# Values of two blocks of keys at a time, ahead of scores, in a two-layer graph attention kernel on one core

## Chip, cores, metric

One core of one Trainium2 chip runs the whole program. The metric is the device time of the execution in microseconds (us), lower is better. PE is the matrix engine (TensorE), DVE the vector engine (VectorE), ACT the scalar engine (ScalarE), POOL the GpSimd engine, SP the engine that issues most DMAs.

## What is computed

Thirty-two graphs of 512 nodes with 512 features go through two layers. The first is a graph sum with two weight matrices, the second is attention with 8 heads of 64, masked by the adjacency matrix. In the kernel's names B is 32, N and D are 512. After each layer the input is added and the rows are normalised.

```python
# layer 0, a = adj as float, deg its row sums
mi = einsum('bkd,od->bko', x, Wi); mj = einsum('bkd,od->bko', x, Wj)
x  = layernorm(x + deg[None, :, None] * (mi + b) + einsum('ij,bjo->bio', a, mj))
# layer 1
q, k, v = heads(h @ Wq.T + bq), heads(h @ Wk.T + bk), heads(h @ Wv.T + bv)
scores  = where(adj == 0, -inf, q @ k.T / sqrt(64))
x  = layernorm(h + merge(softmax(scores) @ v) @ Wo.T + bo)
```

## The kernel before

**Pieces.** Each 512 x 512 weight product is computed by a Strassen-like scheme with seven half-size products ("pieces", `piece`, line 411), numbered 1, 2, 6, 7, 4, 5, 3. The sums of activations that they need are made on POOL by `combos` (line 387); the sums of weights lie in DRAM and come through a ring of seven tiles (`prefetch`, line 274, on SP). A piece is eight 128 x 128 by 256 matrix instructions into one PSUM bank, `mma` or `mmb`; a layer-0 piece ("l0") is twice as long, since it has two weights. The pieces of one product fall into groups that add up in the bank: X is pieces 1 and 2, Y is 6, 7 and 4, Z is 5 and 3. After each piece but the first of a product its bank is read by DVE (`xh`, L445; `v`, L456; `q` and `k`, L465 and L472) or ACT (L454, L470 for piece 2); after the first ACT copies it (`p`, L434). Each bank is single, so the next piece into the same bank waits for that read, whether it adds into the group or opens a new one. This is why the lists alternate between two banks. Kinds: l0 (layer 0), v, q, k, pj (output projection). `l0_gather` (L325) multiplies by the adjacency matrix.

**Attention of one batch row b.** Its eight heads are two groups g of four, and keys are four blocks kc of 128, so a row takes eight steps (`STEPS`). For a step, `scores` (line 477) is called twice, for two heads each: a PSUM tile `sc` of two banks (two such tiles exist), `exp` on ACT in place (L485), then the multiplication by the 0/1 adjacency mask into an SBUF tile `e` on DVE (L486, "the mask"; four `e` tiles exist). `values` (line 496) multiplies the four heads' `e` of one block of keys by v into the two PSUM tiles `ov`. `presum` (line 488) adds the `e` of the four blocks on POOL (kc 1) or DVE (kc 2, 3). At the end of a group `sums` (line 506) makes the row sums with a matrix product into an `sc` tile, `drain` (line 515) copies them to SBUF on ACT, and `rest` (line 540) is seven DVE instructions: four inversions (`invert`, L522), two `scale` (L538, which also frees the `ov` tiles), and one `tell` (L526), a sum for a check.

**Forms of matrix instructions.** By the profile's columns pieces use the array as 128\*128, scores as 64\*128 (two heads side by side), values and sums as 128\*32 (four heads side by side).

**Order.** Nothing is left to a scheduler: under `tc.manual_schedule()` each engine's queue holds its instructions in the order in which the Python code emits them. Period n works on several rows at once: attention of row n-1, layer 0 and q, k, v of row n, the projection of row n-2 (m), and the gather of row n+1. The lists `phase_b`, `phase_c` and `phase_a` hold the pieces and the small tasks between them; `by_steps` (line 684) cuts them into eight steps. With n from 2 to 30 step 0 has l0-2, pj-1, l0-6, pj-2; step 1 l0-7, pj-6, l0-4, pj-7; step 2 l0-5, pj-4, l0-3, pj-5; step 3 v1, pj-3, v2, q1, k1, q2; step 4 k2, q5, v5, q3, v3; step 5 six pieces of q and v; step 6 gathers and k5, k3, k6; step 7 a gather, k7, l0-1, k4. l0, v and k share one bank, pj and q the other; in the gathers' steps the next period's bank for l0 is used.

The loop of the periods (line 765) does, for each step: scores of the step, values of the step before, at a group's end sums, drain and then `rest` kept in `extra`; then the pieces of the step, with the presums and `extra` handed out between them (in step 0 all of `extra` after the first piece, otherwise one or two instructions after each).

**h.** The output h of layer 0 is needed transposed. `stats` (DVE, POOL) and `apply` (ACT, L296) normalise half of the rows, `h_store` (line 356) sends the half to DRAM from ACT's queue, `h_load` (line 362) fetches it with four DMAs on SP's queue, `h_turn` (line 370) transposes it on DVE (L373) into `HT`, from which v, q and k are made. Pieces 1 and 2 of these need only half 0.

Of the kernel before, what the change touches and what calls it, by code (L numbers as in the profile page):

```python
# [25 lines left out]
def gnn_attention_kernel(  # L26
# [37 lines left out]
    B, N, D = x.shape  # L64
    NC = N // P
# [14 lines left out]
    def work(shape, name, bufs, dtype=FT):  # L80
        return pools.work.tile(shape, dtype, name=name, bufs=bufs)
# [7 lines left out]
    def ov_tile():  # L89
        return psum.tile([P, 512], FT, name="ov", bufs=2)  # L90

    def sc_tile():
        return psum.tile([P, 2, N], FT, name="sc", bufs=2)
# [147 lines left out]
    def ring_tile():  # L241
        return work([P, 2, Q], "ring", RING)
# [31 lines left out]
    def prefetch():  # L274
        while len(TILES) < min(len(KEYS), ring.used + RING) and KEYS[len(TILES)] in WS:
            t = ring_tile()
            nc.sync.dma_start(t, WS[KEYS[len(TILES)]])
            TILES.append(t)
# [102 lines left out]
    def quarter(src, j, n):  # L381
        return src[:, 2 * j:2 * j + 2, Q * n:Q * n + Q]

    def ot_quarter(b):
        return lambda j, n: OT[b, j][:, :, Q * n:Q * n + Q]
# [91 lines left out]
    def scores(b, hp, kc):  # L477
        ps = sc_tile()
        for s in range(2):
            r = slice(s * HD, (s + 1) * HD)  # L480
            nc.tensor.matmul(ps[:, s, :], KT[b, hp // 2][r, hp % 2, kc * P:(kc + 1) * P],  # L481
                             QT[b, hp // 2][r, hp % 2, :], start=True, stop=True)
        e = E[hp % 2, kc] = work([P, 2, N], "e", 4)

        nc.scalar.activation(ps, ps, AF.Exp, scale=QSCALE)  # L485
        nc.vector.tensor_tensor(e, ps, edge[:, kc:kc + 1, :].to_broadcast([P, 2, N]), op=OP.mult)  # L486
# [9 lines left out]
    def values(b, g, kc):  # L496

        if kc == 0:
            PV[g] = [ov_tile(), ov_tile()]
        for r in range(2):  # L500
            for h in range(4):
                c0 = (4 * g + h) * HD + 32 * r
                nc.tensor.matmul(PV[g][r][32 * h:32 * h + 32, :], V[b][:, kc, c0:c0 + 32], E[h // 2, kc][:, h % 2, :],  # L503
                                 start=(kc == 0), stop=(kc == NC - 1))

    def sums(g, kcs=(1,), last=1):

        if g not in RL:
            RL[g] = (sc_tile()[:, 0, :], work([P, N], "rl", 1))
        for kc in kcs:  # L510
            for h in range(4):
                src = ES[h // 2] if kc == 1 else E[h // 2, kc]
                nc.tensor.matmul(RL[g][0][32 * h:32 * h + 32, :], ones[:, :32], src[:, h % 2, :], start=(kc == 1), stop=(kc == last))  # L513

    def drain(b, g):

        j = 2 * (b * 2 + g)
        nc.scalar.activation(RL[g][1], RL[g][0], AF.Identity, accum_out=told[:, j:j + 1])
# [21 lines left out]
    def rest(b, g):  # L540
        return [(invert, g, c) for c in range(4)] + [(scale, b, g, 0), (scale, b, g, 1), (tell, b, g)]
# [9 lines left out]
    def z(f, *a):  # L551
        return (0.0, f, *a)

    def pc(kind, b, i, bank):
        return (2 * PC if kind == "l0" else PC, piece, kind, b, i, bank)
# [6 lines left out]
    def banks(n):  # L562

        return ("a", "b") if n % 2 == 0 else ("b", "a")
# [48 lines left out]
    def project(m, i):  # L613

        res = [pc("pj", m, i, banks(m)[1])]
        if i == 1:
            res = [z(combos, TO, m, ot_quarter(m), (1,))] + res
        if i == 2:
            res = [FLUSH] + res + [z(combos, TO, m, ot_quarter(m), (2, 3, 4))]
        return res  # L620

    def phase_b(n):

        m = n - 2
        if m < 0:
            res = []
            side = [z(add_bo, 0, i) for i in range(2)]
            A, K = banks(n)
            for i, bank in ((2, A), (6, K), (5, A), (7, K), (4, K), (3, A)):
                res.append(pc("l0", n, i, bank))  # L630
                if i == 4:
                    res += [z(stats, n, 0)]
                res += side[:1]
                side = side[1:]
            return res + [z(apply, n, 0), z(stats, n, 1), (TR, l0_norm, n, 0), (TR, l0_norm, n, 1)]
        A = banks(n)[0]
        l0 = {i: pc("l0", n, i, A) for i in ORDER}
        return [l0[2], *project(m, 1), l0[6], *project(m, 2), l0[7], z(add_bo, n - 1, 0), *project(m, 6), l0[4], z(stats, n, 0),
                *project(m, 7), z(apply, n, 0), z(h_store, n, 0), l0[5], z(h_load, n, 0), z(add_bo, n - 1, 1), *project(m, 4),
                l0[3], z(stats, n, 1), z(h_turn, n, 0), *project(m, 5)]  # L640

    def phase_c(n):

        m = n - 2
        norm = [(TR, l0_norm, n, ic) for ic in range(NC)]
        h = lambda j, i: quarter(HT[n], j, i)
        A, K = banks(n)
        v, q, k = [{i: pc(kind, n, i, bank) for i in ORDER} for kind, bank in (("v", A), ("q", K), ("k", A))]
        if m < 0:
            res = [v[1]] + ([z(apply, n, 1)] if n else []) + [q[1], v[2], norm[2], norm[3], z(combos, TH, n, h, (1, 2)), k[1],  # L650
                                                             z(combos, TH, n, h, (3, 4)), q[2], k[2]]
        else:
            res = [z(apply, n, 1), z(h_store, n, 1), v[1], *project(m, 3), z(h_load, n, 1), z(stats, m, 0), v[2], z(stats, m, 1),
                   q[1], k[1], z(apply, m, 0), z(h_turn, n, 1), q[2], z(apply, m, 1), z(store, m),
                   z(combos, TH, n, h, (1, 2)), z(combos, TH, n, h, (3, 4)), k[2]]
        side = []
        if n == 0:

            side = [z(graph_forms, 2), None, z(graph_forms, 0), None, z(graph_forms, 1)]
        for i in LATE:  # L660
            for f in q[i], v[i]:
                res += [f] + [g for g in side[:1] if g]
                side = side[1:]
                if i in (6, 7) and 0 < n < B - 1:
                    res += [z(load_xa, n + 1, 2 * (i == 7) + (f is v[i]))]
            if i == 3 and 0 < n < B - 1:
                res += [z(load_x, n + 1)]
            if i == 7 and n + 1 < B:
                res += [z(ahead, n + 1)]
        return res  # L670
# [35 lines left out]
    def run(f):  # L706
        f[1](*f[2:])
# [29 lines left out]
    def flags():  # L737
# [5 lines left out]
        nc.vector.tensor_scalar(again, tot, -1.0, 1.0, op0=OP.mult, op1=OP.add)  # L743

    PERIODS = [first() + phase_c(0) + phase_a(1)]
    half = None
    for n in range(1, B):
        todo = phase_b(n) + phase_c(n) + phase_a(n + 1)
        if n < B - 1:
            half = sum(f[0] for f in todo) / 2  # L750

        PERIODS += [by_steps(todo, half)]
# [8 lines left out]
    for f in PERIODS[0]:  # L761
        run(f)
        if f[1] is combine:
            prefetch()
    for n in range(1, B + 1):
        b = n - 1
        extra = []
        for step in range(STEPS):
            g, kc = divmod(step, NC)
            scores(b, 2 * g, kc)  # L770
            scores(b, 2 * g + 1, kc)
            pb, pg, pk = (b, *divmod(step - 1, NC)) if step > 0 else (b - 1, 1, NC - 1)
            if pb >= 0:
                values(pb, pg, pk)
                if pk == NC - 1:
                    sums(pg, *(((1, 3), 3) if pb == B - 1 else ()))
                    drain(pb, pg)
                    extra = rest(pb, pg)
            late = [(presum, i, kc) for i in range(2) if kc > 0]
            if b == B - 1 and kc > 2 - g:  # L780

                late = []
            for f in PERIODS[n][step]:
                if f is FLUSH:
                    some = len(extra)
                else:
                    run(f)

                    some = 0 if f[0] == 0.0 else len(extra) if step == 0 else max(1, round(f[0] / PC))
                if some:  # L790
                    for g in late[:1] + extra[:some]:
                        g[0](*g[1:])
                    late, extra = late[1:], extra[some:]
            for g in late + extra:
                g[0](*g[1:])
            extra = []
# [19 lines left out]
    with tc.If(flag > 0), tc.tile_pool(name="general", bufs=1) as pools.work:  # L816
# [26 lines left out]
        with tc.For_i(0, B, 1) as b:  # L843
            g = "general"
# [105 lines left out]
```

## Time and profile before

| | us |
|---|---|
| median of 3 runs (3705.42 to 3707.18) | 3706.04 |
| the profiled execution | 3703.08 |
| its span | 3701.0 |
| PE busy | 3664.3 |
| DVE busy | 2390.7 |
| POOL busy | 1938.8 |
| ACT busy | 1028.4 |

The page gives, for each engine, the sum of its instructions' times and their share of the span. The timeline lists instructions in order: start, length, engine, line, operation, what it writes and reads, the number of merged instructions, and in brackets the idle time ahead and what ended it. PE's ends are modelled and overlap the next start, so its rows are best read from start to start. A line of the windows view is one stretch of time: its length, then each engine's busy time with its number of instructions, the granted clock of PE, the DMA share and the rate. One period takes 113.4 us, and its pattern is the same from period 2 on, but for the two banks, which swap.

### The profile page before, as it was taken

The numbers are of one execution on the slowest core, as the hardware profiler recorded it, in microseconds if no ns is written. First come the engines' busy times: TensorE is split into PE (matmuls) and PEld (weight loads), VectorE is DVE, ScalarE is ACT, GpSimd is POOL, SyncE is SP. The second block draws the span as 40 slices with busy tenths as digits, with TensorE's granted clock in tenths as the row PEclk, the third lists the DMA queues.
The fourth block names the chain that finished last, engine by engine and source line by source line (L and its number), as shares of the span: only waits on it lengthen the run. The fifth ranks groups of instructions, "written<-read, shape, count | busy, mean of one in ns | idle before, by whom it ended". The sixth has DMA issues, their size and how long they took to land.

```text
span 3701.0 us, 49651 instructions
## 1 busy us (share of the span) xinstructions
PE 3664.3 (99%) x18474; PEld 2511.5 (68%) x18474; DVE 2390.7 (65%) x3134; ACT 1028.4 (28%) x1482; POOL 1938.8 (52%) x1985
## 2 busy tenths in 40 slices
PE   8999999999999999999999999999999999999998
PEld 5666666666676767676767666666666676767663
DVE  4566766666666666666666666666666666666665
ACT  2222232322322222222232222232222322222322
POOL 3465545555455564455554555545555545555443
PEclk9999999999999999999999999999999999999999
DMA  7444555455564445554555544555544556445541
GB/s 250 127 126 134 151 151 162 122 143 137 154 159 142 128 135 151 157 155 125 137 143 157 159 135 134 137 149 160 148 132 132 147 151 164 124 136 140 151 137 47
DMA packets 797173, 530.02 MB, mean 143 GB/s; under 512 B 530432, under 2 KB 611840, under 8 KB 796928
## 3 DMA queue, kind: packets, MB, share of 16 engines
q1 hardware_dynamic: 780384, 494.78, 49.7%
q10 hardware_dynamic: 16320, 31.46, 2.3%
q8 instruction: 151, 2.47, 0.3%
q14 instruction: 94, 0.77, 0.1%
q0 software_dynamic: 224, 0.53, 0.0%
HBM read 453.25 MB, written 73.40 MB: 142 GB/s over the span
## 4 chain that ended last, share of the span: by engine, by line
PE 96%; DVE 1%; SPq 1%; POOL 1%; DMA 0%; issue 0%; ACT 0%; POOLq 0%; DVEq 0%; ACTq 0%
PE mma L427 31%; PE mmb L427 31%; PE sc L481 13%; PE ov L503 13%; PE mmb L325 3%; PE mma L325 3%; PE sc L513 2%; SPq L113 0%; DVE rl L522 0%; DVE e L486 0%; DMA wv<-e 0%; SPq L144 0%; DVE st L289 0%; PE sc L727 0%; POOL es L492 0%
## 5 line engine op out<-in xcount | busy, mean ns | idle before, releaser
L485 ACT ACTIVATE sc<-sc 128x1024 f32<-128x1024 f32 x512 | 493.2, 1007 | 1552.5 <-PE sc L481 1546.2
L486 DVE TENSOR_TENSOR e<-sc,edge 128x1024 f32<-128x1024 f32 x512 | 602.2, 1217 | 206.3 <-ACT sc L485 174.3
L427 PE MATMUL mmb<-ring,big 128*128 128x256 f32 x3144 | 731.7, 381 | 0.0
L427 PE MATMUL mma<-ring,big 128*128 128x256 f32 x3112 | 725.3, 382 | 4.2 <-ACT p L434 3.1
L427 PEld LDWEIGHTS mmb<-ring,big 128*128 128x128 f32 x3144 | 592.0, 190 | 131.5 <-issue 26.8
L427 PEld LDWEIGHTS mma<-ring,big 128*128 128x128 f32 x3112 | 586.3, 190 | 135.2 <-issue 26.0
L396 POOL TENSOR_TENSOR big<-big 128x512 f32<-128x512 f32 x376 | 492.7, 1338 | 32.4 <-ACT big L354 11.7
L481 PE MATMUL sc<-q,k 64*128 64x512 f32 x2048 | 509.1, 615 | 0.0
L503 PE MATMUL ov<-e,v 128*32 128x512 f32 x4096 | 492.5, 598 | 4.9 <-DVE oT L538 4.9
L492 POOL TENSOR_TENSOR es<-e 128x1024 f32<-128x1024 f32 x128 | 300.0, 2355 | 351.7 <-DVE e L486 351.7
L427 PE MATMUL mma<-big,ring 128*128 128x256 f32 x1808 | 430.3, 381 | 3.2 <-DVE k L465 3.2
L427 PE MATMUL mmb<-big,ring 128*128 128x256 f32 x1776 | 422.8, 381 | 1.0 <-DVE v L456 1.0
L291 POOL TENSOR_SCALAR mv<-mv 128x1 f32<-128x1 f32 x256 | 49.6, 194 | 671.6 <-DVE mv L290 659.1
L427 PEld LDWEIGHTS mma<-big,ring 128*128 128x128 f32 x1808 | 340.5, 190 | 76.5 <-issue 26.0
L427 PEld LDWEIGHTS mmb<-big,ring 128*128 128x128 f32 x1776 | 334.4, 190 | 73.4 <-issue 26.0
L503 PEld LDWEIGHTS ov<-e,v 128*32 128x32 f32 x4096 | 107.0, 109 | 352.2 <-issue 320.8
L204 POOL TENSOR_TENSOR xlo<-xh,xhi 128x512 fp32r<-128x512 f32 x128 | 163.6, 1289 | 337.6 <-ACT xhi L203 337.6
L481 PEld LDWEIGHTS sc<-q,k 64*128 64x128 f32 x2048 | 176.1, 186 | 207.3 <-issue 205.1
L340 POOL TENSOR_TENSOR big<-big,deg_r 128x512 f32<-128x512 f32 x124 | 173.6, 1400 | 266.3 <-DVE big L339 266.3
L494 DVE TENSOR_TENSOR es<-es,e 128x1024 f32<-128x1024 f32 x250 | 304.2, 1217 | 0.0
L445 DVE TENSOR_TENSOR xh<-xh,mma 128x512 f32<-128x512 f32 x186 | 126.6, 681 | 267.0 <-PE mma L427 267.0
L445 DVE TENSOR_TENSOR xh<-xh,mmb 128x512 f32<-128x512 f32 x186 | 126.7, 681 | 263.0 <-PE mmb L427 263.0
(155 smaller groups left out, 3656.2 us busy)
## 6 DMA issues: line engine op xcount, KB each, us to landing
ring<-wo SPq DMA_DIRECT2D x217, 256.0 KB, 2.8
ring<-wq SPq DMA_DIRECT2D x160, 256.0 KB, 3.9
ring<-wv SPq DMA_DIRECT2D x160, 256.0 KB, 3.4
ring<-wk SPq DMA_DIRECT2D x160, 256.0 KB, 3.2
ring<-wi SPq DMA_DIRECT2D x155, 256.0 KB, 2.7
ring<-wj SPq DMA_DIRECT2D x155, 256.0 KB, 2.7
xh<-in_x_dram SPq DMA_DIRECT2D x32, 1024.0 KB, 5.4
xa<-in_x_dram SPq DMA_DIRECT2D x124, 256.0 KB, 4.0
```

What stands on the lines that cost most here:

```text
L204: nc.gpsimd.tensor_sub(lo, xs, hi.bitcast(FT))
L325: nc.tensor.matmul(pm, parts[w][:, jc, :], adjR[:, jc, :], start=(w == 0 and jc == 0), stop=(w == 1 and jc == NC - 1))
L340: nc.gpsimd.tensor_tensor(XD[b][:, dc, :], XD[b][:, dc, :], deg_r, op=OP.mult)
L396: nc.gpsimd.tensor_tensor(dst, p, q, op=OP.subtract)
L427: nc.tensor.matmul(pm[:, c * Q:(c + 1) * Q], lhs, rhs, start=first, stop=(kc == 1 and n == len(terms) - 1), skip_group_check=True)
L445: nc.vector.tensor_tensor(d, d, pm, op=OP.add)
L481: nc.tensor.matmul(ps[:, s, :], KT[b, hp // 2][r, hp % 2, kc * P:(kc + 1) * P], QT[b, hp // 2][r, hp % 2, :], start=True, stop=True)
L485: nc.scalar.activation(ps, ps, AF.Exp, scale=QSCALE)
L486: nc.vector.tensor_tensor(e, ps, edge[:, kc:kc + 1, :].to_broadcast([P, 2, N]), op=OP.mult)
L492: nc.gpsimd.tensor_add(ES[i], E[i, 0], E[i, 1])
L494: nc.vector.tensor_add(ES[i], ES[i], E[i, kc])
L503: nc.tensor.matmul(PV[g][r][32 * h:32 * h + 32, :], V[b][:, kc, c0:c0 + 32], E[h // 2, kc][:, h % 2, :], start=(kc == 0), stop=(kc == NC - 1))
```

## The change

Three edits. In `phase_b`, `apply` and `h_store` of half 0 stand ahead of the piece pj-7 instead of behind it. In `phase_c`, pj-3 and the load of half 1 stand ahead of v1, and the order of the following pieces is v1, q1, v2, q2, k1, k2 (it was v1, v2, q1, k1, q2, k2, with pj-3 behind v1), with the small tasks at other places between them. In the loop, the values of two steps are kept in `due` and done together in every second step (kc 0 and 2), ahead of that step's scores; at a group's end (steps 0 and 4) sums, drain and all of `rest` are emitted there too, ahead of the scores and so ahead of their masks. In the last period, steps 1 to 7 (`alone`) keep the old order.

```diff
         return [l0[2], *project(m, 1), l0[6], *project(m, 2), l0[7], z(add_bo, n - 1, 0), *project(m, 6), l0[4], z(stats, n, 0),
-                *project(m, 7), z(apply, n, 0), z(h_store, n, 0), l0[5], z(h_load, n, 0), z(add_bo, n - 1, 1), *project(m, 4),
+                z(apply, n, 0), z(h_store, n, 0), *project(m, 7), l0[5], z(h_load, n, 0), z(add_bo, n - 1, 1), *project(m, 4),
                 l0[3], z(stats, n, 1), z(h_turn, n, 0), *project(m, 5)]
...
-            res = [z(apply, n, 1), z(h_store, n, 1), v[1], *project(m, 3), z(h_load, n, 1), z(stats, m, 0), v[2], z(stats, m, 1),
-                   q[1], k[1], z(apply, m, 0), z(h_turn, n, 1), q[2], z(apply, m, 1), z(store, m),
+            res = [z(apply, n, 1), z(h_store, n, 1), *project(m, 3), z(h_load, n, 1), v[1], z(stats, m, 0), q[1], z(stats, m, 1),
+                   v[2], q[2], z(apply, m, 0), z(h_turn, n, 1), k[1], z(apply, m, 1), z(store, m),
                    z(combos, TH, n, h, (1, 2)), z(combos, TH, n, h, (3, 4)), k[2]]
...
+    due = []
     for n in range(1, B + 1):
         b = n - 1
         extra = []
         for step in range(STEPS):
             g, kc = divmod(step, NC)
-            scores(b, 2 * g, kc)
-            scores(b, 2 * g + 1, kc)
-            pb, pg, pk = (b, *divmod(step - 1, NC)) if step > 0 else (b - 1, 1, NC - 1)
-            if pb >= 0:
-                values(pb, pg, pk)
-                if pk == NC - 1:
-                    sums(pg, *(((1, 3), 3) if pb == B - 1 else ()))
-                    drain(pb, pg)
-                    extra = rest(pb, pg)
+            alone = b == B - 1 and step > 0
+            if alone:
+                scores(b, 2 * g, kc)
+                scores(b, 2 * g + 1, kc)
+            if alone or kc % 2 == 0:
+
+                for pb, pg, pk in due:
+                    values(pb, pg, pk)
+                    if pk == NC - 1:
+                        sums(pg, *(((1, 3), 3) if pb == B - 1 else ()))
+                        drain(pb, pg)
+                        extra = rest(pb, pg)
+                due = []
+            due.append((b, g, kc))
+            if not alone:
+
+                for f in extra:
+                    f[0](*f[1:])
+                extra = []
+                scores(b, 2 * g, kc)
+                scores(b, 2 * g + 1, kc)
             late = [(presum, i, kc) for i in range(2) if kc > 0]
```

## The prediction

> **What bounds the kernel now.** I read the page's first and fourth parts, then one block's stretch, then PE beside DVE in order of time. TensorE is busy for 99% of the span and is 96% of the chain that ended last:
>
> ```profile
> PE 3664.3 (99%) x18474; PEld 2511.5 (68%) x18474; DVE 2390.7 (65%) x3134; ACT 1028.4 (28%) x1482; POOL 1938.8 (52%) x1985
> ...
> PE 96%; DVE 1%; SPq 1%; POOL 1%; DMA 0%; issue 0%; ACT 0%; POOLq 0%; DVEq 0%; ACTq 0%
> ```
>
> A busy PE could still hide waits, so I took the stretch of one block of batch (it repeats every 113.4 us):
>
> ```profile
> 904.44:1017.88 113.44, 113.44 (x581) 78.47 (x577) 74.33 (x97) 31.90 (x46) 60.67 (x64) 1.00 0.53 144
> ```
>
> PE is busy for the whole 113.44 us; DVE for 74.33. So PE waits for nobody in a block, and only two things can move the time: fewer PE cycles, or a new wait of PE. In PE's timeline I read starts only (ends are modelled):
>
> ```profile
> 941.89 1.89 PE L427 MATMUL mmb<-ring,big 128*128 128x256 f32 x8
> 943.71 1.99 PE L481 MATMUL sc<-q,k 64*128 64x512 f32 x8
> 945.63 1.92 PE L503 MATMUL ov<-e,v 128*32 128x512 f32 x16
> 947.49 1.99 PE L427 MATMUL mma<-ring,big 128*128 128x256 f32 x8
> 949.32 1.89 PE L427 MATMUL mmb<-ring,oT 128*128 128x256 f32 x8
> ...
> 959.96 1.92 PE L503 MATMUL ov<-e,v 128*32 128x512 f32 x16
> 961.70 1.04 PE L513 MATMUL sc<-es,ones 128*32 128x512 f32 x8
> 962.67 1.99 PE L427 MATMUL mma<-big,ring 128*128 128x256 f32 x8
> ```
>
> A piece (8 records) takes 1.73 us in a run of pieces, 1.82 before scores and 1.83 after values. Scores take 1.92, values 1.86 before a piece but 1.74 before sums, which use the same 128*32 form; sums 0.97. Each change of form costs about 0.1 to 0.2 us. DVE's timeline shows what a group's end costs there: four inversions, two scales and a sum (L526), 908.81 to 914.02, is 5.21 us in one run; two masks (L486) take 2.27 to the next start (1002.74 to 1005.01), an eviction 0.69:
>
> ```profile
> 908.81 3.38 DVE L522 RECIPROCAL rl<-rl 128x128 f32<-128x128 f32 x4
> 912.22 1.29 DVE L538 TENSOR_TENSOR oT<-ov,rl 128x512 f32<-128x512 f32 x2
> 913.43 0.67 DVE L526 TENSOR_REDUCE told<-rl 128x1 f32<-128x512 f32 x1
> 914.02 0.68 DVE L445 TENSOR_TENSOR xh<-xh,mma 128x512 f32<-128x512 f32 x1
> ...
> 942.09 0.69 DVE L445 TENSOR_TENSOR xh<-xh,mma 128x512 f32<-128x512 f32 x1 [1.63 <-PE mma L427]
> ...
> 945.68 0.65 DVE L445 TENSOR_TENSOR xh<-xh,mmb 128x512 f32<-128x512 f32 x1
> 946.26 2.34 DVE L486 TENSOR_TENSOR e<-sc,edge 128x1024 f32<-128x1024 f32 x2
> ...
> 963.53 0.95 DVE L522 RECIPROCAL rl<-rl 128x128 f32<-128x128 f32 x1 [0.91 <-ACT rl L518]
> ```
>
> The first inversion starts 1.83 us after sums start (961.70 to 963.53); between them is ACT's drain. Last, what a late eviction does to PE is seen in period 1, where a piece follows another into the same bank:
>
> ```profile
> 133.06 3.72 PE L427 MATMUL mma<-ring,big 128*128 128x256 f32 x16
> 137.56 3.72 PE L427 MATMUL mma<-ring,big 128*128 128x256 f32 x16 [0.78 <-DVE xh L445]
> ```
>
> The double piece takes 3.45 (3.55 after a change of form or a stop), so 136.61 was due; the eviction, 136.81 to 137.50, held it to 137.56: 0.06 after the eviction's end.
>
> [...] the eviction at 914.02 stood behind the seven instructions since 908.81. [...] the waits below are up to 2.1 us, and the block's clock is 1.00, so I price no throttling.
>
> **The change, part by part.**
>
> *Fewer changes of form.* Two steps now hold pieces, values, values, scores, pieces, scores, pieces: five changes instead of six. An entry into values and an exit go. The exit is 1.86 - 1.74 = 0.12; the entry about 0.02 (1.74 against four passes of 0.43). The new neighbours (pieces to values, values to scores) are not in the trace; bounds 0.10 and 0.20 a pair, I take 0.15. With 31 blocks of four pairs: 124 x 0.15 = -19 us (-12 to -25).
>
> *Inversions ahead of masks.* In steps 0 and 4, PE now does values, values, sums, scores. From the step's start: values at 0 and 1.74, sums 3.47, scores 4.44, pieces 6.36. The second scores reuse the PSUM slot of sums, so they wait for the drain, which ends about 1.8 after sums start (5.27); they are due near 5.4: no cost, at most 0.1. DVE's queue is now seven instructions of the group's end, then masks, then the evictions of pieces. Inversions start at 3.47 + 1.83 = 5.30, the end is 5.21 later, 10.51, masks are done at 12.78, and only then the first DVE eviction starts. Before, masks came first and the inversions lay after or between pieces' evictions.
>
> Step 0, n = 2 to 31: l0-2 (double) 6.36 to 9.91, pj1 to 11.64, then l0-6 opens a new tile in l0-2's bank. That eviction is 12.78 to 13.47, so l0-6 starts at 13.53: 1.89 late, and 0.10 for starting again, 1.99. 30 x 1.99 = +60 us.
>
> Step 4, n = 1 to 31: k2 6.36 to 8.19, q5 to 9.92, v5 to 11.65, then q3 adds into q5's bank. q5's two-part eviction (0.87) is 12.78 to 13.65, q3 starts at 13.71: 2.06 late, 2.16 with the restart. v5 waits only for k2's eviction, which ACT does behind two exponentials (to 7.5) and two normalisations, until about 9.9: just in time. 31 x 2.16 = +67 us. If q3's first half waits only for the eviction's first half, 0.44 less: 53.
>
> *h stored sooner, used one piece later.* The store half 0 now stands on ACT ahead of step 2's exponentials; the load on SP is where it was, after l0-5 and its prefetches, which in this trace is what it follows (937.39, 0.7 after l0-5), not the store. So it gains nothing. But pj3 is moved to be the first piece of step 3, while pj5 is the last of step 2, in the same bank and group. DVE has, from pj5's start at 941.89: l0-3's eviction, four statistics, h's transpose, then pj5's eviction, ending 946.33, 4.44 later. Before, v1 in the other bank stood between. Now step 3 has no values, so pj3 is due at 1.82 + 1.92 = 3.74 and may start at 4.50: 0.76 late. 30 x 0.76 = +23 us. If the transpose waits longer for its DMA, more; if statistics were earlier, nothing. The second half's load keeps its distance from its store (7.96 after step 3's start), and its transpose (ending some 1.7 into step 4) lies ahead of the inversions that wait till 5.30. k1 and k2 in one bank are parted by values and scores: nothing.
>
> *Cover that values gave.* Step 7 loses 1.86 us of values. DVE has masks, a transpose, two bias additions, a presum, then k7's eviction, ending 9.24 after scores start (1000.52 to 1009.76). k4 in that bank is due at 1.92 + 1.96 + 1.73 + 3.45 = 9.06, may start at 9.30: 0.24 + 0.10 = 0.34 late. 29 x 0.34 = +10 us; between 0 and 1 us each. In steps 1 and 5 the same sum leaves 0.2 us and more in hand.
>
> *Tail.* Step 0 of the last period has one piece; step 1's scores need the first mask, about 11.8 after the start against 8.3 due: 3.5, where before a wait of 1.2 stood (3623.17). +2.
>
> Everything else is equal: same pieces, same prefetch, the presums end before the masks that overwrite their inputs (GpSimd done some 8 us earlier by my count).
>
> Sum: 60 + 67 + 23 + 10 + 2 - 19 = +143. The profiled execution took 3703.08 us around a span of 3701.0; 3703 + 143 = 3846. The median of the runs is 3 us above it: 3849.
>
> **Rivals.**
>
> *Half of it (0.17).* Evictions release PE by halves and steps 3 and 7 have more slack than counted: 60 + 53 + 2 - 19 = +96, 3802. For: step 7's 0.24 us is within small shifts. Against: 946.33 and 1009.76 are chains without an idle moment.
>
> *More of it (0.15).* The late masks are passed on: the drain holds the second scores and step 1's and 5's pieces meet a still late DVE, 1 us more at each of 61 group ends: +61, 3910. For: DVE has only 39 us free in a block. Against: in steps 1 and 5 masks are due 2.2 after scores, when the evictions left over are one or two.
>
> *The other side (0.05): DVE isn't late.* If the group's end lies in DVE's idle time, all stops vanish and the drains saved are left: 3706 - 19 = 3687. It decides if masks are done 2.1 us sooner, that is if the end takes 3.1 us instead of 5.21, and pj5's and k7's evictions come 0.8 sooner. For: DVE is busy only 65%. Against: the inversions cannot start before 5.30, and 5.21 is a row of the trace. The drain alone can't turn the sign: all changes of form of two steps are 2 x 0.53 = 1.06 us, 131 us in all, under the 160 of stops.
>
> *The change doesn't do what it says (0.03).* If the queue isn't the program's order, masks pass the inversions and little is left, about 3706. Every DVE row above stands in program order.
>
> **How the numbers follow.** The forecast has 0.60; its own range is 3815 to 3885 (each stop 0.3 either way, drain 12 to 25). The range 3785 to 3900 takes in the half case and a part of the larger one. A measurement of this kernel can tell about 0.2%. Slower: 0.60 + 0.17 + 0.15 and a little of the rest, 0.93; faster 0.05; same 0.02.
>
> **What would show it.** Right: in steps 0 and 4, seven DVE instructions ahead of L486; an idle PE of about 2 us at l0-6 and at q3, released by L445 and L472; 0.8 at pj3; values 1.74 apart. Wrong: a block still without idle PE, or a block not near 113.4 + 4.6 = 118 us.

## The result, and the profile after

The changed kernel takes 3898.69 us (3897.76 to 3901.96, 5 runs) against 3706.29 us of the kernel before on the same chip: a ratio of 1.0522, 95% interval 1.0507 to 1.0536. It is slower, as forecast, and by more than the 3849 us that were forecast; the time lies just inside the upper edge of the range, 3900.

The page after, parts 1 and 4:

```profile
PE 3705.9 (95%) x18474; PEld 2535.8 (65%) x18474; DVE 2382.9 (61%) x3134; ACT 1035.9 (27%) x1482; POOL 1950.2 (50%) x1985
...
PE 58%; DVE 19%; POOL 14%; issue 5%; ACT 2%; SPq 1%; DMA 1%; DVEq 0%; POOLq 0%; ACTq 0%
```

PE runs the same 18474 instructions, is now idle for about 5% of the span, and the chain that ended last goes through DVE and POOL for a third of it. Two of PE's numbers have to be read together: the span grew by 195.9 us, PE's busy time grew too, by 41.6. So there is more than waiting: some instructions take longer.

Two neighbouring periods in the windows view (length, busy times of PE, PEld, DVE, ACT, POOL, clock, DMA share, GB/s):

```profile
945.60:1065.67 120.07, 115.39 (x578) 79.70 (x577) 74.10 (x97) 32.16 (x46) 61.11 (x63) 0.99 0.49 136
1065.67:1183.90 118.23, 113.53 (x577) 78.52 (x576) 74.10 (x97) 32.16 (x46) 60.98 (x62) 1.00 0.50 138
```

Both were 113.4. The second line ends 0.16 us before its period does (the next pair of values starts at 1184.06), so the period takes 118.39 us; the first has 1.7 us more, and the clock of PE isn't 1.00 in it. First the stops, that is, the times in which PE waits. PE's timeline after, step 3's start, then step 4, with its pair of values, sums and scores ahead:

```profile
993.08 1.99 PE L481 MATMUL sc<-q,k 64*128 64x512 f32 x8
995.76 1.99 PE L427 MATMUL mmb<-ring,oT 128*128 128x256 f32 x8 [0.69 <-DVE xh L445]
...
1006.32 3.64 PE L503 MATMUL ov<-e,v 128*32 128x512 f32 x32
1009.77 1.04 PE L513 MATMUL sc<-es,ones 128*32 128x512 f32 x8
1010.75 2.01 PE L481 MATMUL sc<-q,k 64*128 64x512 f32 x8
1012.68 1.99 PE L427 MATMUL mma<-big,ring 128*128 128x256 f32 x8
1014.51 1.89 PE L427 MATMUL mmb<-big,ring 128*128 128x256 f32 x8
1016.24 1.89 PE L427 MATMUL mma<-ring,big 128*128 128x256 f32 x8
1020.08 3.47 PE L427 MATMUL mmb<-big,ring 128*128 128x256 f32 x8 [1.95 <-DVE q L472]
1023.34 2.15 PE L427 MATMUL mma<-ring,big 128*128 128x256 f32 x8
```

DVE's timeline beside it (the brackets give the idle time ahead and what ended it):

```profile
1011.60 3.39 DVE L522 RECIPROCAL rl<-rl 128x128 f32<-128x128 f32 x4 [2.87 <-ACT rl L518]
1015.09 1.29 DVE L538 TENSOR_TENSOR oT<-ov,rl 128x512 f32<-128x512 f32 x2
1016.30 0.68 DVE L526 TENSOR_REDUCE told<-rl 128x1 f32<-128x512 f32 x1
1016.89 2.35 DVE L486 TENSOR_TENSOR e<-sc,edge 128x1024 f32<-128x1024 f32 x2
1019.15 0.87 DVE L472 SCALAR_TENSOR_TENSOR q<-mmb,bq_c,p 128x256 f32<-128x256 f32 x2
```

The reader sees the queue that was forecast: inversions 1.83 us after sums start (1009.77 to 1011.60), masks 5.29 later, q5's eviction 2.26 later still, done at 1020.02; q3, due at 1016.24 + 1.73 = 1017.97, starts at 1020.08. Each of these is within 0.1 us of its forecast. pj3, due at 993.08 + 1.92 = 995.00, starts at 995.76: 0.76 late, as forecast.

Step 0 of the same period, PE and then DVE:

```profile
955.52 1.89 PE L427 MATMUL mmb<-ring,oT 128*128 128x256 f32 x8
959.21 3.69 PE L427 MATMUL mma<-ring,big 128*128 128x256 f32 x16 [1.80 <-POOL big L396]
...
956.17 2.35 DVE L486 TENSOR_TENSOR e<-sc,edge 128x1024 f32<-128x1024 f32 x2
958.43 0.68 DVE L445 TENSOR_TENSOR xh<-xh,mma 128x512 f32<-128x512 f32 x1
```

l0-6 is due at 955.52 + 1.73 = 957.25 and starts at 959.21, 1.96 late and 0.10 after the end of l0-2's eviction (L445) behind the masks; 1.89 were forecast. The view names a POOL instruction here; the experiment with the two stops swapped shows why it can't be that one.

What was not forecast is q3's own length: from its start to the next piece's it takes 3.26 us, where 1.83 were due. Shorter windows show why:

```profile
1016.00:1020.00 4.00, 2.13 (x10) 1.51 (x8) 4.00 (x7) 0.01 (x1) 0.00 (x0) 1.00 0.93 274
1020.00:1021.00 1.00, 0.93 (x3) 0.81 (x4) 0.62 (x2) 0.00 (x0) 0.00 (x0) 0.72 1.06 410
1021.00:1022.00 1.00, 1.00 (x3) 0.79 (x3) 0.00 (x0) 0.00 (x0) 0.00 (x0) 0.50 0.86 328
1022.00:1023.00 1.00, 1.00 (x4) 0.76 (x3) 0.00 (x0) 0.00 (x0) 0.00 (x0) 0.50 0.00 0
1023.00:1024.00 1.00, 1.00 (x4) 0.82 (x3) 0.42 (x2) 0.00 (x0) 0.00 (x0) 0.58 0.00 0
```

The column before the last two is the granted clock: it is halved from about 1020.4 to 1023.8, 3.41 us, right behind the stop. In the clock record such stretches within the periods have this length or, once, twice it, and they start at whole multiples of 3.413 us from each other (from the one in period 1 to those of periods 2 to 30: 70, 105, 175, 245 and so on). Sixteen of the 29 step 4s of periods 2 to 30 have one, no step 0 has.

To see where all the time went I took, from the starts of scores in each trace, the length of each step (from scores to the next step's scores), as medians over periods 2 to 30, with the time lost by a halved clock taken off:

```
step                 0      1      2      3      4      5      6      7    period
before             15.24  14.33  14.33  14.33  13.46  14.33  14.69  12.73  113.44
after              14.54  16.05  12.47  17.66  12.96  16.05  12.83  15.82  118.38
after, no stops*   12.47  16.05  12.47  16.90  10.75  16.05  12.83  15.30  112.82
stop                2.07   0      0      0.76   2.21   0      0      0.52    5.56
```

\* summed from rows of the trace before: scores 1.92, pieces 1.73, double pieces 3.45, 0.10 for an entry into pieces, 0.09 for leaving them, a pair of values 3.57, with sums 4.43. Steps 6 and 7 are the ones before less 1.86 of values; a pair counts to the step that ends with it, so step 7 has the 4.43 of values and sums ahead of step 0's scores, step 3 that of step 4.

From the same starts and the clock record: periods 2 to 30 grew by 174.1 us in all, of which 27.3 are a halved clock and 146.8 the stops less what the fewer changes of form save (the prediction's "drains"). Period 1 grew by 11.7 (3.4 of it clock; the 2.7 us of values and sums that now fall ahead of the last scores counted are taken off), period 31 by 6.0 and the last by 3.2 (1.7 of each clock). That is the whole 195.9 but for 0.9.

### The profile page after: what moved, and what is told of

Same layout as the page of the kernel before. It is cut to its first block, busy times and chain, and to the rows that moved or that the text cites. A ratio compares the mean times of both kernels' runs of the same rounds, so it can differ in the third digit from the quotient of the medians.

```text
span 3896.9 us, 49717 instructions
## 1 busy us (share of the span) xinstructions
PE 3705.9 (95%) x18474; PEld 2535.8 (65%) x18474; DVE 2382.9 (61%) x3134; ACT 1035.9 (27%) x1482; POOL 1950.2 (50%) x1985
## 4 chain that ended last, share of the span: by engine, by line
PE 58%; DVE 19%; POOL 14%; issue 5%; ACT 2%; SPq 1%; DMA 1%; DVEq 0%; POOLq 0%; ACTq 0%
PE mma L427 20%; PE mmb L427 20%; PE ov L503 9%; PE sc L481 6%; POOL big L396 6%; DVE e L486 4%; DVE xh L345 3%; POOL xh L442 3%; DVE rl L522 3%; POOL xlo L204 2%; POOL big L340 2%; DVE es L494 2%; DVE oT L538 1%; DVE xh L445 1%; DVE big L339 1%
## 5 line engine op out<-in xcount | busy, mean ns | idle before, releaser
L396 POOL TENSOR_TENSOR big<-big 128x512 f32<-128x512 f32 x376 | 492.6, 1337 | 79.4 <-DVE big L373 50.2
L427 PE MATMUL mma<-big,ring 128*128 128x256 f32 x1808 | 442.7, 388 | 39.8 <-DVE q L472 29.2
L427 PE MATMUL mmb<-big,ring 128*128 128x256 f32 x1776 | 440.6, 392 | 35.8 <-DVE q L472 29.2
L503 PE MATMUL ov<-e,v 128*32 128x512 f32 x4096 | 466.9, 595 | 3.1 <-DVE oT L538 3.1
L522 DVE RECIPROCAL rl<-rl 128x128 f32<-128x128 f32 x252 | 213.4, 909 | 227.6 <-ACT rl L518 227.6
L204 POOL TENSOR_TENSOR xlo<-xh,xhi 128x512 fp32r<-128x512 f32 x128 | 176.7, 1391 | 340.1 <-ACT xhi L203 340.1
L503 PEld LDWEIGHTS ov<-e,v 128*32 128x32 f32 x4096 | 119.7, 109 | 278.5 <-issue 274.1
L296 ACT ACTIVATE xh<-xh,mv 128x512 f32<-128x512 f32 x252 | 194.2, 809 | 370.6 <-POOL mv L293 370.6
```

The costliest lines, as they stand in the source:

```text
L204: nc.gpsimd.tensor_sub(lo, xs, hi.bitcast(FT))
L296: nc.scalar.activation(y, y, AF.Identity, bias=mv[:, 4:5], scale=mv[:, 3:4])
L396: nc.gpsimd.tensor_tensor(dst, p, q, op=OP.subtract)
L427: nc.tensor.matmul(pm[:, c * Q:(c + 1) * Q], lhs, rhs, start=first, stop=(kc == 1 and n == len(terms) - 1), skip_group_check=True)
L522: nc.vector.reciprocal(RL[g][1][:, c], RL[g][src][:, c])
```

## The experiments

My theory (A): the place of the masks behind the group's end makes the stops of steps 0 and 4; pj5 and pj3 in one bank make that of step 3, lost cover that of step 7; and the clock is halved because of the length of step 4's stop. Rivals: pairs of values ahead of scores cost by themselves (B), the new lists do (C), something else than the stop halves the clock (D), DVE's queue doesn't set the stops (E).

### The group's end between the pieces again

```diff
-                for f in extra:
-                    f[0](*f[1:])
-                extra = []
                 scores(b, 2 * g, kc)
```

> The changed kernel, but the group's end on DVE (inversions, scales, the sum for the check) is handed out between the pieces as before, so masks stand ahead of it again; pairs of values and the new lists stay. Theory A (the masks' place behind the group's end makes the stops of steps 0 and 4, and the stop of step 4 halves PE's clock): both stops go, PE's clock is full throughout, the stops at pj3 (0.76 x 30 = 23 us) and k4 (0.5 x 29 = 15 us) stay, the drains saved are 0.15 x 124 = 18 us: about 3706 + 23 + 15 - 18 = 3726 us. Rival B (pairs of values ahead of scores cost by themselves, since scores come 3.6 us later in a step): over 3800 us. Rival C (the lists of h and of pieces cost most): 3890 us.

Measured: 3744.76 us, ratio 1.0104 (1.0088 to 1.0119). So 154 of the change's 192 us are the place of the group's end. Step 4 on PE and DVE:

```profile
978.10 1.89 PE L427 MATMUL mmb<-big,ring 128*128 128x256 f32 x8
979.83 1.89 PE L427 MATMUL mma<-ring,big 128*128 128x256 f32 x8
981.55 1.89 PE L427 MATMUL mmb<-big,ring 128*128 128x256 f32 x8
```

```profile
976.55 2.35 DVE L486 TENSOR_TENSOR e<-sc,edge 128x1024 f32<-128x1024 f32 x2 [4.18 <-ACT sc L485]
978.82 0.94 DVE L522 RECIPROCAL rl<-rl 128x128 f32<-128x128 f32 x1
980.03 0.88 DVE L472 SCALAR_TENSOR_TENSOR q<-mmb,bq_c,p 128x256 f32<-128x256 f32 x2 [0.26 <-PE mmb L427]
```

Masks first, q5's eviction at 980.03, and q3 (981.55) 1.72 after v5: no stop. Steps 0 and 4 take 12.55 and 10.77 us, and no halving is left in step 4. B and C fall: with pairs and lists kept, the time is far below the 3800 and 3890 us that they asked for. The 19 us above the 3726 expected: about 7 are in the first period. The first period's list of pieces is another one: layer 0's transposes on PE use the two PSUM tiles of scores, so without values between they wait for masks and for normalised rows (in the changed kernel PE is idle 1.88 us there for rows from ACT and 1.57 us for a mask). About 11 are in periods 2 to 30 (steps 0, 3 and 5 are on average 0.08 to 0.16 us longer than counted), the rest at the end.

### The pairs alone

The loop as in the experiment above, with the lists of before.

> The kernel before with the pairs of values (and sums and drain) ahead of scores alone: old lists, the group's end between the pieces. Theory A: no stop in steps 0 and 4, none at pj3 (v1 stands ahead of it; v1 itself may wait 0.2 us for h's transpose, 6 us in all), k4's stop of step 7 stays (15 us), drains saved 18 us: 3709 us, between 3700 and 3715. Rival B: over 3780 us. If all that is saved and nothing waits: 3688 us.

Measured: 3756.21 us, ratio 1.0139 (1.0124 to 1.0155), 47 us over theory A. Step 3 is not steady here but takes 17.4 to 20.8 us (1.7 of the longest are a halved clock). What holds it, in this kernel's timeline (all engines):

```profile
1066.87 0.37 ACTq L360 DMA_DIRECT2D hd<-xh  x1
...
1068.00 0.38 SPq L277 DMA_DIRECT2D ring<-in_wvT_dram  x1
...
1070.56 2.91 SPq L367 DMA_DIRECT2D xa<-hd  x4
...
1077.87 1.25 DVE L373 STREAM_TRANSPOSE big<-xa 128x1024 f32<-128x1024 f32 x1 [2.26 <-DMA xa<-hd]
...
1079.22 1.97 PE L427 MATMUL mmb<-ring,big 128*128 128x256 f32 x8 [2.43 <-issue]
```

The load of h's half 0 lands late, its transpose waits 2.26 us, and v1 starts 0.1 us after the transpose ends. The rows point to the store of h. It (L360) stands on ACT behind step 2's exponentials, and step 2's pieces now follow its scores at once. So the load (L367) starts 3.69 us after the store and 2.18 after the prefetch ahead of it (L277) ends; in the trace before these were 3.46 (933.93 to 937.39) and 0.10. With the new lists (the first experiment) the store stands 6.28 ahead of the load (1058.41 to 1064.69), and the load follows its prefetch by 0.11. This is read from rows; no run moved the store alone. Before, there were also the 1.86 us of values between scores and v1. So the edit that uses h one piece later earns 11 us in this loop (3756.21 against 3744.76): it trades a varying wait at v1 for the steady 0.76 at pj3. My expectation had the transpose's data on time because the trace before had it so.

### The lists alone

The loop of before, with the two lists of the change.

> The kernel before with the new lists alone (apply and h_store ahead of pj7; pj3 ahead of v1, the order v1, q1, v2, q2, k1, k2); the loop is the old one. Theory A: the 1.86 us of values between scores and pj3 cover the late eviction of pj5 (0.76), so no stop: 3706 us within 4. Rival C (the lists cost by themselves): 3728 us or more.

Measured: 3703.36 us, ratio 0.9996 (0.9988 to 1.0005): no change, each step as before to 0.01 us. The lists cost and bring something only where values don't stand between scores and pieces.

### The check's sum later

```diff
-                for f in extra:
+                for f in extra[:-1]:
                     f[0](*f[1:])
-                extra = []
+                extra = extra[-1:]
```

> The changed kernel, but the last of the seven DVE instructions of a group's end (the sum for the check, 0.59 us to the next start) comes after the first piece, so behind the masks. Theory A: each of 61 stops is 0.59 us shorter (-36 us); and if PE's clock is halved because the stop of step 4 (2.1 us) empties more than about half of one of the throttle's windows of 3.41 us, at 1.5 us it is no longer halved (-34 us): 3829 us. Rival D (the clock is halved for another cause, as the long stretch of 128*32 values or the sums, and not for the stop's length): 3863 us, with as many halvings as now (19 inside the periods). Rival E (the stops are not set by DVE's queue): 3899 us.

Measured: 3884.36 us, ratio 1.0495 (1.0479 to 1.0511). Step 0 takes 13.94 us instead of 14.54, the 0.60 expected; step 4 stays at 12.96. The experiment was put wrongly for step 4: there the sum came behind k2, still ahead of q5's eviction, so that stop was not shortened, and most of 37.5 us that a halved clock costs are lost there. It supports the account of step 0's stop (against E), and says nothing on D, as step 4's stop kept its length.

### The new loop with the old lists

> The changed kernel with the lists of before: the new loop alone (pairs, and the group's end ahead of masks). Theory A: the stops of steps 0 and 4 and the halved clock stay as they are; in step 3 pj3's stop of 0.76 goes, but v1, now first, waits for the transpose of h's half 0, which waits for its load (0 to 2.5 us, as with pairs alone, where step 3 took 17.4 to 20.8): 3905 to 3915 us. Rival C (the new lists cost more than they bring): 3876 us or less.

Measured: 3897.83 us, ratio 1.0522 (1.0506 to 1.0538), 7 us under the expectation and the same as the changed kernel. The lists bring nothing here that can be told: step 3's median is 17.89 against 17.66, 7 us in 29 periods, but the clock lost 27.3 us in all instead of 34.1, 7 us less (13 halvings in periods 2 to 30 instead of 16). That the clock made up for the lists is chance as far as these runs show.

### One stop shorter, the other longer

In step 4 the check's sum goes to the end of the step; in step 0 it is done twice ahead of the masks (its second value is the same).

```diff
+                held = extra[-1:] if step == 4 else []
+                for f in extra[:-1] if held else extra:
+                    if f[0] is tell:
+                        j = 2 * (f[1] * 2 + f[2]) + 1
+                        nc.vector.reduce_sum(told[:, j:j + 1], RL[f[2]][1], axis=AX.X)
                     f[0](*f[1:])
...
-            for g in late + extra:
+            for g in late + extra + held:
                 g[0](*g[1:])
```

> The changed kernel with the two stops changed in length and nothing else: in step 4 the sum for the check comes at the end of the step (stop 0.59 us shorter, about 1.5), in step 0 it is done twice ahead of the masks (stop 0.59 us longer, about 2.6). The sums of the lengths are the same. Theory A (a stop of over about 2 us within one window of 3.41 us halves the clock in the next): no halving in step 4 any more, halvings in step 0, about as many or more; in all within 30 us of 3899. Rival D (something in step 4 other than the stop's length halves the clock): halvings stay in step 4, none in step 0.

Measured: 3900.84 us, ratio 1.0528 (1.0509 to 1.0547). The halvings moved: step 0 loses 29.0 us by them in the whole run (0 in the changed kernel), step 4 1.7, in period 1 alone (32.1 in the changed kernel). Of periods 2 to 30, sixteen of the 29 step 0s have one, no step 4. Step 0 in this kernel, PE's timeline and windows:

```profile
1073.92 1.89 PE L427 MATMUL mma<-ring,oT 128*128 128x256 f32 x8
1078.34 5.29 PE L427 MATMUL mmb<-ring,big 128*128 128x256 f32 x16 [2.52 <-POOL big L396]
1083.46 1.89 PE L427 MATMUL mma<-ring,oT 128*128 128x256 f32 x8
```

```profile
1076.00:1078.00 2.00, 0.00 (x0) 0.00 (x0) 2.00 (x3) 0.44 (x1) 2.00 (x3) 1.00 0.72 243
1078.00:1081.00 3.00, 2.66 (x6) 2.19 (x7) 0.24 (x1) 0.00 (x0) 3.00 (x3) 0.53 0.01 3
```

l0-6 takes 5.12 us instead of 3.55, at a clock of 0.53. D falls: it is the stop's length, and where the stop falls (see the last section).

The view names a POOL instruction (L396, 1076.27 to 1077.54) as the stop's end. It can't be what PE waits for: with the group's end between the pieces (the first experiment) l0-6 starts ahead of the same POOL instruction:

```profile
1037.16 3.62 PE L427 MATMUL mmb<-ring,big 128*128 128x256 f32 x16
1037.78 1.28 POOL L396 TENSOR_TENSOR big<-oT 128x512 f32<-128x512 f32 x1
```

In the kernel with the stops swapped the eviction on DVE ends at 1078.24, 0.10 before PE goes on.

### Pairs without the stops

Two versions: the group's end between the pieces, v1 ahead of pj3 again, h's half 0 loaded ahead of l0-5 and transposed ahead of the statistics, the second bias addition behind k7, and the old order in the first block:

```diff
-            if i in (1, 2):
-                res += [z(base, n, i - 1)]
+            if i in (1, 3):
+                res += [z(base, n, i // 2)]
...
-                z(apply, n, 0), z(h_store, n, 0), *project(m, 7), l0[5], z(h_load, n, 0), z(add_bo, n - 1, 1), *project(m, 4),
-                l0[3], z(stats, n, 1), z(h_turn, n, 0), *project(m, 5)]
+                z(apply, n, 0), z(h_store, n, 0), *project(m, 7), z(h_load, n, 0), l0[5], z(add_bo, n - 1, 1), *project(m, 4),
+                l0[3], z(h_turn, n, 0), z(stats, n, 1), *project(m, 5)]
...
-            alone = b == B - 1 and step > 0
+            alone = b in (0, B - 1) and step > 0
```

> Pairs of values ahead of scores, the group's end between the pieces, and the four stops taken away that the runs showed: v1 ahead of pj3 again, h's half 0 loaded ahead of l0-5 and transposed ahead of the statistics of half 1; the second bias addition of layer 0 behind k7 instead of ahead of it; the first block keeps the old order. Theory A: a period is 113.43 - 0.59 and little else (0.2 us in steps 0 and 5 as with the rest between pieces): 3705 - 29 x 0.4 + 3 in the last two periods = 3697 us, between 3688 and 3702. If h's load is still late or POOL is: 3705 to 3730 us.

Measured: 3703.84 us, ratio 0.9996 (0.9988 to 1.0004): no change, 7 us over the expectation. The stops of 2.07, 0.76, 2.21 and 0.52 are gone; steps 3, 5 and 7 take 17.12, 16.19 and 15.30, so 0.22 and 0.14 are left in steps 3 and 5. The second version takes these away. It also puts back the bias addition in the first period, whose step 7 takes 13.81 us, 2.9 more than before; I took that for a loss.

```diff
-            if i in (1, 3):
+            if i in (1, 2 if n <= 2 else 3):
...
-            res = [z(apply, n, 1), z(h_store, n, 1), v[1], *project(m, 3), z(h_load, n, 1), z(stats, m, 0), v[2], z(stats, m, 1),
+            res = [v[1], z(apply, n, 1), z(h_store, n, 1), *project(m, 3), z(h_load, n, 1), z(stats, m, 0), v[2], z(stats, m, 1),
...
+                if step == 4:
+                    f = extra.pop(0)
+                    f[0](*f[1:])
                 scores(b, 2 * g, kc)
```

> The version before this one (early h) with its three small stops taken away: in step 3 v1's copy on ACT stands ahead of the normalisation of half 1 (0.22 us a period), in step 4 one inversion stands ahead of the masks, in the time in which they wait for the exponentials anyway, so that less of the group's end is left for step 5 (0.14 us a period), and the second bias addition of row 2, in the first period, is where it was (2.9 us). Theory A: the drains saved are all that is left: 3704 - 6.4 - 4 - 2.9 = 3691 us, 3686 to 3697, faster than before by 0.2 to 0.5%. Rival F (what is left in steps 0, 3 and 5 is the price of the new order itself, as the wait of the second scores for the drain): 3701 to 3704 us.

Measured: 3691.67 us, ratio 0.9965 (0.9951 to 0.9978): faster than the kernel before, by the changes of form that are saved. A period takes 112.91 us; steps 3 and 5 are at 16.90 and 16.05. Of the 2.9 us in the first period only 0.2 came back (13.59): the other 2.7 are no loss, but the values and sums at the turn to period 2, which now come ahead of the scores from which I count. So the expectation was met for a reason that is in part another: the 10 us of steps 3 and 5, and 3.7 us less in the last two periods. Rival F falls with it. The page's first line is that of a kernel bound by PE again:

```profile
PE 3651.3 (99%) x18474; PEld 2519.3 (68%) x18474; DVE 2395.8 (65%) x3134; ACT 1036.4 (28%) x1482; POOL 1987.1 (54%) x1985
```

PE's busy time is 13.0 us below the 3664.3 of before, with the same instructions.

## Why the prediction was right, and where its size was off

**Changes of form (the prediction's "drains").** Forecast 0.15 us a pair. The last version saves 113.44 - 112.91 = 0.53 a period, 0.13 a pair, and still has 0.08 of waiting in step 0; PE is busy for 99% of the span in both kernels and runs the same instructions. The table's sums, which have no waiting at all, give 0.62, 0.155 a pair; that is a sum from rows and not a measurement. Right, and shown by the last version. What PE does at a change of form isn't shown, only what it costs.

**Steps 0 and 4.** Forecast 1.99 and 2.16; measured 2.07 and 2.21. The group's end was the cause: giving it back its place removes both but for 0.08 in step 0. That q3 waits for the whole of q5's eviction, and not its first half, is seen in the trace (start 0.06 after the end of both parts).

**h and the lists.** pj3's 0.76 was exact. That the lists gain nothing was right in the old loop. Its reason, that the load follows the prefetch and not the store, held by 0.1 us only. The prediction missed that in the new loop the store moves closer to the load and the load becomes late, so that v1 first would have waited instead; with the group's end between the pieces the lists earn 11 us.

**Step 7.** Forecast 0.34; measured 0.52.

**The term that was missed: the clock.** The prediction said "the waits below are up to 2.1 us, and the block's clock is 1.00, so I price no throttling". It cost 34.1 us by the clock record, 27.3 of them in periods 2 to 30. That waits of up to 2.1 us leave the clock alone was not shown by the trace before: the 1.00 came from a period in which PE is busy for all of its 113.44 us, so it says nothing of stops. In these runs 1.94 to 1.95 us idle inside one window of 3.413 us were enough. In the profiled execution the miss is 196 - 143 = 53 us. Beside the clock it holds the first period, 8.3 us without clock where 1.6 were counted because I took its list to be like the others (7), step 7's underestimate (29 x 0.18 = 5), and small excesses in steps 0, 3 and 4 of periods 2 to 30 (7).

**Rivals.** "More of it" named the right size (3910) by a wrong mechanism: in steps 1 and 5 nothing was passed on (16.05, no stop). So it is luck that the time lies inside the range: the forecast's own range ended at 3885, the room up to 3900 was left for this rival, and a clock that nobody had counted filled it. "Half of it" fell with q3, which waited for the whole eviction. The other side fell: DVE was as late as the rows said, and these rows stand in program order, seven instructions ahead of the masks.

## What to carry to other kernels

In this kernel PE has no idle time in a period (113.44 of 113.44 us before), and the order that saves it changes of form paid only where each engine that frees its banks stayed on time: 3691.67 us without the stops, 3898.69 with them, 3706.29 before. Put work that waits for a late result (here inversions that wait for sums and drain) behind the work that PE's next banks need, and look at what the moved matrix instructions had been hiding where they stood. In this kernel step 4's stop of 2.2 us cost 0.94 more in clock on average (27.3 us in 29 periods), 1.7 where it was halved; price a stop with that too, and check the first and last periods by their own lists.

## What the runs showed of the hardware

The clock of PE was halved for 3.413 us at a time, on a grid of windows of that length, behind stops that didn't fill a window (in steps 0 and 4 they held 1.94 to 2.53 us of one). Which stops bring it can be read from the traces. I cut four of them into windows of 3.413 us, counted from the start of a halving, and took, for the longest stop of each step 0 and each step 4 in periods 2 to 30, the largest part that lies in one window (idle time of PE as the profile gives it):

| run | step | length of most stops, us | periods with the stop whole in one window, of 29 | halvings right behind that window | largest part, halved | largest part, not halved |
|---|---|---|---|---|---|---|
| the changed kernel | 0 | 1.80 | 9 | 0 | | up to 1.81 |
| | 4 | 1.95 | 18 | 16 | 1.94 to 1.95 | up to 1.95 |
| the check's sum later | 0 | 1.21 | 16 | 0 | | up to 1.21 |
| | 4 | 1.95 | 20 | 18 | 1.95 | up to 1.95 |
| the old lists | 0 | 1.80 | 7 | 0 | | up to 1.93 |
| | 4 | 1.95 | 15 | 13 | 1.94 to 1.95 | up to 1.94 |
| stops swapped | 0 | 2.52 | 9 | 16 | 2.09 to 2.53 | up to 1.95 |
| | 4 | 1.35 | 10 | 0 | | up to 1.35 |

All 63 halvings follow a window that holds 1.94 us or more of the stop, and none of the 169 other stops has more than 1.95 in one window. So the point lies at 1.94 to 1.95 us of a window of 3.413 here, 57% of it, and the halving takes the next window. Step 4's stop of 1.95 is right on it: it counts only where it falls whole into a window. Step 0's 1.80 wasn't enough even there, while 2.52 could also be cut by a window's edge and still count. What ends a halving isn't read here: the one of period 1 in the changed kernel went on for a second window, though its first held only 0.9 us of idle time.

Each halving shifts what follows it: periods with one and without take 120.07 and 118.39 us in the changed kernel, and their mean over periods 2 to 30, 119.44, is close to 35 windows (119.46). That the periods and the grid lock to each other isn't shown. With the check's sum later the mean is 118.92, and periods 8 to 16 go without a halving.
